# The offset convolution as four products per two columns, one on each strip of the array, in a bottleneck kernel with deformable sampling

## The chip, the cores and the metric

The kernel runs on one core of one Trainium2 chip. The metric is the device time in microseconds of one execution of the whole program. A profiled execution also has a span, from its first to its last instruction. TensorE (PE) multiplies matrices, VectorE (DVE) and ScalarE (ACT) do elementwise work and read PSUM, GpSimd (POOL) does elementwise work on SBUF, and SyncE (SP) issues the DMAs.

## The reference

The input is 64 images of 1024 channels by 14 x 14 points, in float32. Two residual blocks follow each other. The first is an ordinary bottleneck with batch normalisation. The second, where the change lies, is a bottleneck whose middle convolution samples its input at learned offsets:

```python
out = relu(group_norm(conv(x, w1)))                    # 1x1, 1024 -> 256 channels
om = conv(out, w_off, pad=1) + b_off                   # 3x3, 256 -> 27 channels: the offset convolution
off_x, off_y, mask = om[:, :9], om[:, 9:18], sigmoid(om[:, 18:])
py, px = grid_y + off_y, grid_x + off_x                # one point for each of 9 taps
sampled = bilinear_sample(out, py, px) * mask          # 9 samples for each output point
out = einsum('bckhw,ock->bohw', sampled, w2)           # 9 x 256 -> 256 channels
out = relu(group_norm(out))
out = relu(group_norm(conv(out, w3)) + x)              # 1x1, 256 -> 1024 channels
```

## The kernel before

Images go in 32 pairs: one tile has 128 channels on the partitions and two images of 196 points (392 columns) in a row. The first block takes about the first third of the span. After it `build_second_bottleneck` runs with `path = BANDED`: the 14 output rows fall into three groups (rows 0 to 6, 6 to 8, 8 to 14), and the nine taps into two sets, `tapsets` 0 with five taps and 1 with four. (`FULL`, for offsets of more than two points, is in the program and is not taken here.)

The second block is a pipeline over pairs. `fill` does the front work of pairs 0 and 1 and most of that of pair 2; then `slot(t)` runs for t = 0 to 31. In a slot in the middle, in this order on PE:

- `d1`: `first_conv` of pair t+1, 16 products of 392 columns (L1057).
- `sp[0]` woven with the first half of `d3`: `sampling` of pair t for tap set 0 (L1277) and `third_conv` of pair t-1 (L1412). Sampling multiplies the transposed activations `aT` with a matrix of weights `S`, which says how much of each source point each sample takes. `third_conv` makes 4 blocks j of 7 products m of 196 columns. ACT copies a bank to E (m = 1, L1416); DVE adds V from the next (m = 3, L1419); POOL adds twice from V (m = 4, L1424); DVE adds the results z at m = 5 (L1426) and m = 6 (L1431), and takes the group statistics of both results by `third_stats` (L953) right behind each.
- `om`: `offset_conv` of pair t+1 (L1102), then `selection`.
- `sp[1]` woven with the rest of `d3`: `sampling` for tap set 1, then the last two blocks of `third_conv`.
- `pd[0]` and `pd[1]`: `second_conv` of pair t over the samples, 36 products of 392 columns (L1306), with the normalisations, transposes, `factors` and `residual` put between them.

PE's order is this written order. Between `fill` and the last slot, the order on DVE, ACT, POOL and of the DMAs on SP comes from a planner with costs of its own; `keep_in_program_order` keeps marked instructions of an engine in the written order.

The offset convolution has 27 output channels, padded to 32, so it needs only a strip of 32 columns of the 128 x 128 array. There are 18 products (two halves of the channels, nine taps) of all 392 columns, and successive ones go to successive strips, so four partial sums lie in four quarters of a PSUM bank from the pool `ps`, which has three banks and also serves `first_conv`, `third_conv` and the transposes. The products read a zero-bordered copy `pad` of the activations, which POOL makes behind the ReLU on ACT (L1080, L1089). ACT and DVE add the four quarters (L1112, L1114, L1117).

The sampling weights come out of `om`: over several DMAs and elementwise steps, `factors` leaves distances `wd` in DRAM; `spread` broadcasts them into S (weights over rows, L1239) and X (weights over columns, L1235), three DMAs each for a tap set; `corners` multiplies S by X on DVE (L1257), and `sampling` takes the product. `lend` copies parts of `aT` (L1210), `store` writes z out (L1503), and `load` brings pair t+2 (L195, L201). The samples go to the tiles `sm0` and `sm1`, which ACT writes (L1285) and `second_conv` reads.

Of the kernel before, what the change touches and what calls it, by code (L numbers as in the profile page):

```python
# [10 lines left out]
FP = mybir.dt.float32  # L11
AF = mybir.ActivationFunctionType
ALU = mybir.AluOpType
# [31 lines left out]
def kernel(  # L45
# [818 lines left out]
    make_identity(nc, ident)  # L864


    woff_sb = const.tile([P, MB, T, 32], FP, tag="woff", name="woff_sb")
    nc.gpsimd.memset(woff_sb, 0.0)
    for c in range(MB):
        nc.sync.dma_start(woff_sb[:, c, :, :27], woff[ts(c, P)])  # L870
    boff_sb = const.tile([P, 1], FP, tag="boff", name="boff_sb")
    nc.gpsimd.memset(boff_sb, 0.0)
    nc.sync.dma_start(boff_sb[:27], boff)
# [18 lines left out]
    def build_second_bottleneck(l1, path, run, early):  # L892
# [36 lines left out]
        for s in range(2):  # L929
            for h0, h1, _ in groups:  # L930
                for i in range(2):
# [1 line left out]
                        base_sb[:, s, cols(h0, h1)].rearrange("p (i q) -> p i q", i=2)[:, i],  # L933
                        rows(base[:, s, :], h0, h1)[:, i].rearrange("(k r) q -> r k q", k=T),
                    )
        pad = one.tile([P, MB, 2, H + 2, W + 2], FP, tag="pad", name=f"pad{run}")
        nc.gpsimd.memset(pad, 0.0)

        class Norm:

# [132 lines left out]
        def first_norm(p):  # L1073
            q = pairs[p]

            def relu(c, i):
                n, a1 = q["gn1"], q["a1"]

                tc.keep_in_program_order(
                    nc.scalar.activation(  # L1080
                        a1[:, c, ts(i, HW)],
                        a1[:, c, ts(i, HW)],
                        AF.Relu,
                        bias=n.sh[:, c, i : i + 1],
                        scale=n.sc[:, c, i : i + 1],
                    )
                )
                if i == 1:
                    nc.gpsimd.tensor_copy(pad[:, c, :, 1 : H + 1, 1 : W + 1], images(a1[:, c, :]))  # L1089

            return [lambda: q["gn1"].mean(), lambda: q["gn1"].finish()] + [
                lambda c=c, i=i: relu(c, i) for c in range(MB) for i in range(2)
            ]

        def offset_conv(p):
            q = pairs[p]

            def step(n):
                if n == 0:
                    q["po"] = ps.tile([P, N2], FP, tag="ps", name=f"om_{p}")  # L1100
                c, k = divmod(n, T)
                nc.tensor.matmul(  # L1102
                    images(q["po"][ts(n % 4, 32), :]),
                    woff_sb[:, c, k, :],
                    window(pad, c, k),
                    start=(n < 4),
                    stop=(n >= MB * T - 4),
                )
                if n == MB * T - 1:

                    om = one.tile([P, N2], FP, tag="om", name=f"om_{p}")[:32]
                    nc.scalar.activation(om, q["po"][:32], AF.Identity, bias=boff_sb[:32])  # L1112
                    for j in (1, 2):
                        nc.vector.tensor_tensor(om, q["po"][ts(j, 32)], om, ALU.add)  # L1114
                    q["om"] = one.tile([32, N2], FP, tag="off", name=f"off_{p}")
                    for h0, h1, _ in groups:
                        nc.vector.tensor_tensor(  # L1117
                            q["om"][:, cols(h0, h1)].rearrange("p (i q) -> p i q", i=2),
                            rows(q["po"][96:], h0, h1),
                            rows(om, h0, h1),  # L1120
                            ALU.add,
                        )

            return [lambda n=n: step(n) for n in range(MB * T)]

        def selection(p):

# [25 lines left out]
        def factors(p):  # L1153
# [9 lines left out]
            def end():  # L1163
                wt = q["wt"]
                tc.keep_in_program_order(
                    nc.vector.tensor_tensor(wt[:, 0, :], wt[:, 0, :], q["mk"], ALU.mult)
                )

                q["wd"] = {}
                for s in (1, 0):  # L1170
                    for n, gs in alike.items():
                        if s:
                            t = dbounce.tile(
                                [2, len(gs), H, T, n], FP, tag=f"wd{n}", name=f"wd_{p}_{n}"
                            )
# [7 lines left out]
                q["S"], q["sm"] = {}, {}  # L1183

            return [distances, end]

# [34 lines left out]
                    yield g, r0, slice(off, off + n)  # L1221
                    off += n

        def spread(p, e):

            q = pairs[p]
            k0, k1 = tapsets[e]
            S, X = (
                one.tile([QR, wide * KT[e % 2]], FP, tag=f"{v}{e % 2}", name=f"{v}_{p}_{e}")
                for v in ("S", "X")  # L1230
            )
            for g, r0, piece in pieces(e):
                wd = q["wd"][g]
                shape = [R, W, piece.stop - piece.start]
                nc.sync.dma_start(  # L1235
                    X[:, piece],
                    wd[1, :, k0:k1, :].rearrange("r k n -> r (k n)").unsqueeze(0).to_broadcast(shape),
                )
                nc.sync.dma_start(  # L1239
                    S[:, piece],  # L1240
                    wd[0, r0 : r0 + R, k0:k1, :]
                    .rearrange("r k n -> r (k n)")
                    .unsqueeze(1)
                    .to_broadcast(shape),
                )
            q["S"][e] = S, X

        def corners(p, e):

            q = pairs[p]  # L1250
            S, X = q["S"][e]
            k0, k1 = tapsets[e]
            q["S"][e] = {}
            for g, r0, piece in pieces(e):
# [6 lines left out]
        def sampling(p, e):  # L1261
# [5 lines left out]

            def step(turn, g, h0, h1, chunks, c, i0, ni):
                if turn == 0:
                    q["sm"][e] = one.tile(  # L1270
                        [P, MB, KT[e % 2], 2, HW], FP, tag=f"sm{e % 2}", name=f"sm_{p}_{e}"
                    )
                n = (h1 - h0) * W
                pt = ps_s.tile([P, ni, kt, n], FP, tag="ps_s", name=f"sp_{p}_{e}_{g}_{c}_{i0}")
# [113 lines left out]
        def third_conv(p):  # L1388


            q = pairs[p]

            def step(j, m):
                if j == m == 0:
                    first_of_third(p)
# [24 lines left out]
                elif m == 4:  # L1420
                    V, E = q["V"], q["E"]

                    for o, b in ((E[:, 1], E[:, 1]), (z[1][:, HW:], V[:, 1])):
                        tc.keep_in_program_order(nc.gpsimd.tensor_tensor(o, V[:, 0], b, ALU.add))  # L1424
                elif m == 5:
                    nc.vector.tensor_tensor(  # L1426
                        z[0].rearrange("p (i n) -> p i n", i=2), bank, q["E"], ALU.add
                    )
                    third_stats(p, j)
                elif m == 6:  # L1430
                    nc.vector.tensor_tensor(z[1][:, :HW], bank[:, 1], q["V"][:, 0], ALU.add)  # L1431

                    tc.keep_in_program_order(third_stats(p, HB + j))

            return [lambda j=j, m=m: step(j, m) for j in range(HB) for m in range(7)]

# [97 lines left out]
        def slot(t):  # L1534
# [14 lines left out]
            d3 = part(back, third_conv, t - 1)  # L1549

            for e in range(2, E):
                sp[e - 2].append(lambda e=e: this and (spread(t, e), corners(t, e)))
# [13 lines left out]
            if d1:  # L1566
# [1 line left out]
                    d1, norm2 + weights[:1], (4, 7, 12, 12, 13, 13, 14, 10) if back else (10,)  # L1568
                )
                todo += put(weave(sp[0], d3[:half]), norm1, (4, 7, 14, 16, 18, 21))  # L1570
                todo += d3[half : half + 2]
                todo += put(om, weights[1:], (2,))
                todo += weave(sp[1], d3[half + 2 :])
            else:
                todo = put(sp[0], norm2 + weights[1:], (2, 5, 8, 9, 10, 10, 10, 7) if back else (7,))
                todo += put(weave(sp[1], d3[:half]), norm1, (1, 5, 10, 12, 14, 16))
                todo += put(d3[half:], om, (2,) * len(om))
            more = t + 2 < NP and not (early and t < 1)

            extra = [(3, s) for s in norm3[:1]]  # L1580
# [82 lines left out]
        def fill():  # L1663

            for p in range(3):
                start(p)
            load_h3(2, Z0)
            steps = first_conv(0, by_inputs=True)
            steps += put(
                first_conv(1),  # L1670
                first_norm(0) + [lambda: residual(2)] + offset_conv(0) + selection(0) + factors(0),
                (3, 6, 7, 7, 7, 7, 8) + (12,) * (MB * T) + (12, 16, 16),
            )
            steps += [lambda e=e: spread(0, e) for e in range(min(2, len(tapsets)))]
            steps += transposes(0, nc.scalar.copy) + [lambda: lend(0)]
            steps += put(
                first_conv(2),
                first_norm(1) + [lambda: corners(0, 0)] + offset_conv(1) + selection(1),
                (1, 4, 7, 7, 8, 8, 11) + (12,) * (MB * T) + (14,),
            )  # L1680
            for step in steps:
                step()
# [94 lines left out]
```

## Time and profile before

| what | value |
| --- | --- |
| time, median of 3 runs (lowest, highest) | 2985.78 us (2984.6, 2987.03) |
| the profiled execution: its time, its span | 2987.49 us, 2985.7 us |
| mean granted TensorE clock | 0.993 |
| busy: PE, DVE, ACT, POOL | 2926.6, 2069.0, 1191.8, 941.8 us |
| one slot in the middle, from the first product of L1057 to the next slot's | 61.39 us |
| of it busy: PE, DVE, ACT, POOL | 61.39, 38.79, 29.15, 13.95 us |

The busy time of a group is the time in which at least one of its instructions ran, so the mean duration of one instruction is longer than its share of the busy time where instructions overlap. One float32 product stands in the records as two matmuls. A line with an L is a line of the kernel before.

### The profile page before, as it was taken

What the parts mean: (1) busy time and instruction counts of PE and PEld (TensorE: products, weight loads), DVE (VectorE), ACT (ScalarE), POOL (GpSimd) and SP (SyncE); (2) the same over time, 40 slices, a digit from 0 to 9 for tenths busy, and PEclk for the clock granted to TensorE, in tenths of its full rate; (3) what the DMA queues carried; (4) which work ended last, traced back from release to release, by engine and by line L of the source; (5) the groups of instructions that cost most, each with busy time, mean ns of one, the idle gap of its engine ahead of it and who ended that gap; (6) DMA issues with size and microseconds to landing.
All of it is one profiled execution on the core that took longest, in us unless ns stands there. A gap on an engine that the chain in (4) does not pass through costs nothing.

```text
span 2985.7 us, 35773 instructions
## 1 busy us (share of the span) xinstructions
PE 2926.6 (98%) x11269; PEld 1821.8 (61%) x11269; DVE 2069.0 (69%) x5324; ACT 1191.8 (40%) x2504; POOL 941.8 (32%) x1004
## 2 busy tenths in 40 slices
PE   9999899989999999999999999999999999999997
PEld 5555555545555456666666666666666666666664
DVE  7877999997888456666566666666666665666655
ACT  0000222215555434445444454444444454444543
POOL 4621466655664012222222212222122222222121
PEclk9999999999999999999999999999999999999998
DMA  7654000015664436444554455444554445544531
GB/s 230 193 173 141 15 0 1 1 60 186 221 225 182 138 111 189 144 139 153 179 180 131 142 161 185 162 139 144 170 187 141 139 156 177 179 134 142 163 125 45
DMA packets 350411, 424.08 MB, mean 142 GB/s; under 512 B 27876, under 2 KB 292612, under 8 KB 349956
## 3 DMA queue, kind: packets, MB, share of 16 engines
q1 hardware_dynamic: 350212, 421.71, 43.6%
q8 instruction: 91, 1.49, 0.2%
q14 instruction: 108, 0.88, 0.1%
HBM read 296.63 MB, written 116.76 MB: 138 GB/s over the span
## 4 chain that ended last, share of the span: by engine, by line
PE 62%; DMA 1%; DVE 1%; SPq 0%; POOL 0%; ACT 0%; issue 0%; ACTq 0%; DVEq 0%; POOLq 0%
PE pd L1306 24%; PE sp L1277 13%; PE d L1057 10%; PE d L1412 10%; PE om L1102 3%; PE tr L1196 1%; DMA aT<-aT 1%; DMA S<-wd 0%; PE d L1460 0%; DMA wd<-wt 0%; POOL gn_0sc L1003 0%; SPq L1239 0%; DVE gn_0st L953 0%; PE gn_0p L978 0%; SPq L1235 0%
## 5 line engine op out<-in xcount | busy, mean ns | idle before, releaser
L1306 PE MATMUL pd<-sm,w2b_sb 128*128 128x392 f32 x2304 | 791.7, 494 | 0.0
L1306 PEld LDWEIGHTS pd<-sm,w2b_sb 128*128 128x128 f32 x2304 | 424.6, 190 | 267.9
L1277 PE MATMUL sp<-S,aT 126*128 126x420 f32 (+3 forms) x1536 | 490.7, 417 | 10.7 <-DVE S L1257 5.6
L1285 ACT COPY sm<-sp 128x336 f32<-128x336 f32 (+3 forms) x640 | 289.7, 453 | 257.5 <-PE sp L1277 249.2
L1057 PE MATMUL d<-h,w1b_sb 128*128 128x392 f32 x1024 | 357.2, 498 | 0.8 <-ACT h L224 0.8
L530 PE MATMUL c<-v,u_sb 128*128 128x392 f32 x1024 | 342.9, 497 | 11.0 <-DVE bn1sh L167 8.2
L530 PEld LDWEIGHTS c<-v,u_sb 128*128 128x128 f32 x1024 | 194.5, 191 | 159.3 <-issue 11.7
L1277 PEld LDWEIGHTS sp<-S,aT 126*128 126x128 f32 x1536 | 258.0, 191 | 25.7 <-ACT sm L1285 11.1
L1057 PEld LDWEIGHTS d<-h,w1b_sb 128*128 128x128 f32 x1024 | 189.2, 190 | 127.8 <-ACT h L224 2.9
L1493 ACT ACTIVATE z<-z,gn_0sh 128x196 f32<-128x196 f32 x504 | 182.7, 445 | 149.8 <-DVE gn_0sh L1019 134.0
L516 DVE TENSOR_TENSOR v<-t 128x392 f32<-128x392 f32 x256 | 193.1, 812 | 0.0
L1003 POOL TENSOR_TENSOR gn_0sc<-gn_0sc,mhalf 128x16 f32<-128x16 f32 (+3 forms) x35 | 94.6, 2702 | 285.6 <-DVE gn_0sc L1002 274.6
L1412 PE MATMUL d<-h,w3b_sb 128*128 128x196 f32 x744 | 180.4, 332 | 0.7 <-DVE z L1426 0.7
L1424 POOL TENSOR_TENSOR E<-V,E 128x196 f32<-128x196 f32 x124 | 74.1, 598 | 339.2 <-ACT sm L1285 186.7
L1485 DVE SCALAR_TENSOR_TENSOR z<-z,gn_0sc,h 128x196 f32<-128x196 f32 x504 | 178.5, 415 | 0.0
L1257 DVE TENSOR_TENSOR S<-S,X 126x840 f32<-126x840 f32 (+1 forms) x192 | 159.6, 883 | 25.1 <-DMA S<-wd 25.1
L1412 PEld LDWEIGHTS d<-h,w3b_sb 128*128 128x128 f32 x744 | 132.9, 189 | 51.5 <-issue 19.7
L953 DVE BATCH_NORM_STATS2 gn_0st<-z 128x6 f32<-128x196 f32 x504 | 157.4, 354 | 9.9 <-ACT z L1462 2.7
L385 PE MATMUL c<-xc,w1a_sb 128*128 128x392 f32 x384 | 149.1, 497 | 5.2 <-DMA xc<-in_x_dram 5.2
L224 ACT ACTIVATE h<-h,bn3sh 128x392 f32<-128x392 f32 x256 | 140.9, 622 | 11.6 <-DVE h L212 11.6
L212 DVE SCALAR_TENSOR_TENSOR h<-h,bn3sc,h 128x392 f32<-128x392 f32 x256 | 140.6, 620 | 0.0
L718 DVE BATCH_NORM_STATS2 st<-o 128x6 f32<-128x392 f32 x256 | 127.9, 555 | 14.9 <-ACT o L749 8.4
(810 smaller groups left out, 4345.0 us busy)
## 6 DMA issues: line engine op xcount, KB each, us to landing
xc<-in_x_dram SPq DMA_DIRECT2D x128, 392.0 KB
h<-o SPq DMA_DIRECT2D x64, 784.0 KB
h<-in_x_dram SPq DMA_DIRECT2D x64, 784.0 KB
h<-h SPq DMA_DIRECT2D x64, 784.0 KB
out_dram<-z SPq DMA_DIRECT2D x126, 392.0 KB
X<-wd SPq DMA_DIRECT2D x64, 413.4 KB
S<-wd SPq DMA_DIRECT2D x64, 413.4 KB
X<-wd SPq DMA_DIRECT2D x64, 330.8 KB
```

The costliest lines, as they stand in the source:

```text
L385: nc.tensor.matmul(acc[m], a, b, start=(j == 0), stop=(j == HB - 1))
L516: nc.vector.tensor_tensor(v[:, u].rearrange("p (i y x) -> p i y x", y=7, x=7), cols[c][:, :, i : i + 13 : 2, :], cols[c][:, :, j : j + 13 ...
L530: nc.tensor.matmul(m[u], u_sb[:, c, u, k % 4, ts(o, P)], vts[k][c][:, u], start=(c == 0), stop=(c == MB - 1),)
L953: last = nc.vector.bn_stats(self.st[:, b, i, :], src[:, ts(i, HW)])
L1057: nc.tensor.matmul(q["pt"][o], w1b_sb[:, c, ts(o, P)], q["y"][:, c, :], start=(c == 0), stop=(c == CB - 1),)
L1257: nc.vector.tensor_tensor(S[:, piece], S[:, piece], X[:, piece], ALU.mult)
L1277: nc.tensor.matmul(pt[:, i], q["aT"][:, i0 + i, c, starts.index(r0), :], q["S"][e][g, r0][:, :, i0 + i, :], start=(j == 0), stop=(j == len ...
L1285: nc.scalar.copy(dst, pt.rearrange("p i k n -> p k i n"))
L1306: nc.tensor.matmul(q["pd"][o], w2b_sb[:, c, k, ts(o, P)], q["sm"][e][:, c, k - k0].rearrange("p i q -> p (i q)"), start=(k == 0 and c == 0 ...
L1412: nc.tensor.matmul(bank[:, m % 2 if m < 6 else 1], a, b, start=(m < 6), stop=True, skip_group_check=True)
L1485: nc.vector.scalar_tensor_tensor(z[:, ts(i, HW)], z[:, ts(i, HW)], n.sc[:, b, i : i + 1], q["y"][:, o, ts(i, HW)], ALU.mult, ALU.add,)
L1493: nc.scalar.activation(z[:, ts(i, HW)], z[:, ts(i, HW)], AF.Relu, bias=n.sh[:, b, i : i + 1])
```

## The change

The offset convolution is written as F(2,3) along the width: for two neighbouring output columns and three taps of a row, four products of transformed inputs with transformed weights take the place of six. A product now has 98 column pairs of each of two images, 196 columns, for the middle row of taps and 182 for the other two; there are 24 instead of 18, and the four of one tap row go to the four strips. Their accumulators lie in a bank of `second_conv`'s (tag `pd0`) instead of one of `ps`.

`transform` makes the four transformed inputs of a channel half by four DVE instructions of 168 or 196 elements behind the ReLU, and a small POOL copy for the edge columns; the POOL copies to `pad` go. `offset_weights` transforms the weights once, by six DVE instructions, in `fill`. Behind the products ACT makes one copy of 196 columns with the bias, and DVE two additions of 196 columns and six smaller ones that write even and odd columns.

X and the transformed input u get no tiles of their own: X of a tap set goes to the start of that set's sample tile (`sm0`, `sm1`), and u to the second half of `sm1`. So `spread` is split. `spread_rows` brings S as before. `spread_columns` brings X, and its DMAs have to wait until `second_conv` has read the samples of the pair before: for tap set 1 it stands behind `pd[1]`, at the end of the slot. Lending and storing now come before that.

`third_conv` takes the statistics of block j at m = 4 of block j+1, and those of the last block at its end. In `slot` the second `corners` stands ahead of the third block of `third_conv` and of `om`, instead of behind the second product of `om`; in the slots without `d1` the order is put together anew.

The diff, cut; "..." marks what is left out.

```diff
-    woff_sb = const.tile([P, MB, T, 32], FP, tag="woff", name="woff_sb")
-    nc.gpsimd.memset(woff_sb, 0.0)
+    goff = const.tile([P, MB * T, 32], FP, tag="goff", name="goff")
+    woff_sb = const.tile([P, 4, MB * 3, 32], FP, tag="woff", name="woff_sb")
+    nc.gpsimd.memset(goff, 0.0)
     for c in range(MB):
-        nc.sync.dma_start(woff_sb[:, c, :, :27], woff[ts(c, P)])
+        nc.sync.dma_start(goff[:, ds(c * T, T), :27], woff[ts(c, P)])
+    def offset_weights():
+        g0, g1, g2 = (goff.rearrange("p (n k) o -> p n k o", k=3)[:, :, k] for k in range(3))
+        w1, w0, w2, w3 = (woff_sb[:, n] for n in range(4))
+        nc.vector.tensor_tensor(w0, g0, g2, ALU.add)
+        nc.vector.tensor_scalar(w0, w0, 0.5, None, ALU.mult)
+        nc.vector.scalar_tensor_tensor(w1, g1, 0.5, w0, ALU.mult, ALU.add)
+        nc.vector.scalar_tensor_tensor(w2, g1, -0.5, w0, ALU.mult, ALU.add)
+        nc.vector.tensor_scalar(w0, g0, -1.0, None, ALU.mult)
+        nc.vector.tensor_copy(w3, g2)
...
-        pad = one.tile([P, MB, 2, H + 2, W + 2], FP, tag="pad", name=f"pad{run}")
-        nc.gpsimd.memset(pad, 0.0)
...
+        shared = len(tapsets) == 2
+        transformed = {}
...
-                    nc.gpsimd.tensor_copy(pad[:, c, :, 1 : H + 1, 1 : W + 1], images(a1[:, c, :]))
+                    transform(p, c)
...
+        def room(p):
+            if p not in transformed:
+                if shared:
+                    t = sample_buffer(1, f"u_{p}")[:, wide * KT[1] :]
+                else:
+                    t = one.tile([P, MB * 4 * HW], FP, tag="U", name=f"u_{p}")
+                transformed[p] = t
+            return transformed[p].rearrange("p (c n i q) -> p c n i q", c=MB, n=4, i=2)
+        def transform(p, c):
+            u = room(p)[:, c]
+            rows = pairs[p]["a1"][:, c].rearrange("p (r w) -> p r w", w=W)
+            even, odd = rows[:, :, 0::2], rows[:, :, 1::2]
+            half = W // 2
+            for n, (j0, j1, a, b, op) in enumerate(
+                (
+                    (1, half, odd[:, :, 1:], odd[:, :, :-1], ALU.subtract),
+                    (0, half - 1, even[:, :, :-1], even[:, :, 1:], ALU.subtract),
+                    (0, half, even, odd, ALU.add),
+                    (0, half, odd, even, ALU.subtract),
+                )
+            ):
+                dst = u[:, n].rearrange("p i (h w) -> p (i h) w", w=half)
+                nc.vector.tensor_tensor(dst[:, :, j0:j1], a, b, op)
+            n = HW + half - 1
+            edge = u.rearrange("p n i q -> p (n i q)")[:, : 2 * n].rearrange("p (n q) -> p q n", n=2)
+            nc.gpsimd.tensor_copy(edge[:, : HW - 1 : half], rows[:, :, 1 : W - 1 : W - 3])
         def offset_conv(p):
             q = pairs[p]
+            half = W // 2
             def step(n):
+                c, k = divmod(n, 3)
+                k = (1, 0, 2)[k]
                 if n == 0:
-                    q["po"] = ps.tile([P, N2], FP, tag="ps", name=f"om_{p}")
-                c, k = divmod(n, T)
-                nc.tensor.matmul(
-                    images(q["po"][ts(n % 4, 32), :]),
-                    woff_sb[:, c, k, :],
-                    window(pad, c, k),
-                    start=(n < 4),
-                    stop=(n >= MB * T - 4),
-                )
-                if n == MB * T - 1:
+                    q["po"] = ps_d.tile([P, N2], FP, tag="pd0", name=f"om_{p}")[:, :HW].rearrange(
+                        "p (i q) -> p i q", i=2
+                    )
+                u = room(p)
+                o0, o1 = (half if k == 0 else 0), (H - 1 if k == 2 else H) * half
+                i0 = o0 + (k - 1) * half
+                for m in range(4):
+                    nc.tensor.matmul(
+                        q["po"][ts(m, 32), :, o0:o1],
+                        woff_sb[:, m, 3 * c + k, :],
+                        u[:, c, (2, 0, 3, 1)[m], :, i0 : i0 + o1 - o0],
+                        start=(n == 0),
+                        stop=(n == 3 * MB - 1),
+                    )
+                if n == 3 * MB - 1:
                     om = one.tile([P, N2], FP, tag="om", name=f"om_{p}")[:32]
-                    nc.scalar.activation(om, q["po"][:32], AF.Identity, bias=boff_sb[:32])
-                    for j in (1, 2):
-                        nc.vector.tensor_tensor(om, q["po"][ts(j, 32)], om, ALU.add)
+                    m1, m0, m2, m3 = (
+                        q["po"][ts(m, 32)].rearrange("p i q -> p (i q)") for m in range(4)
+                    )
+                    even, odd = om[:, :HW], om[:, HW:]
+                    nc.scalar.activation(even, m1, AF.Identity, bias=boff_sb[:32])
+                    nc.vector.tensor_tensor(odd, even, m2, ALU.subtract)
+                    nc.vector.tensor_tensor(even, even, m2, ALU.add)
                     q["om"] = one.tile([32, N2], FP, tag="off", name=f"off_{p}")
                     for h0, h1, _ in groups:
-                        nc.vector.tensor_tensor(
-                            q["om"][:, cols(h0, h1)].rearrange("p (i q) -> p i q", i=2),
-                            rows(q["po"][96:], h0, h1),
-                            rows(om, h0, h1),
-                            ALU.add,
-                        )
-            return [lambda n=n: step(n) for n in range(MB * T)]
+                        dst = q["om"][:, cols(h0, h1)].rearrange("p (i q n) -> p i q n", i=2, n=2)
+                        for n, (a, b, op) in enumerate(((even, m0, ALU.add), (odd, m3, ALU.subtract))):
+                            a, b = (
+                                v.rearrange("p (i q) -> p i q", i=2)[:, :, h0 * half : h1 * half]
+                                for v in (a, b)
+                            )
+                            nc.vector.tensor_tensor(dst[:, :, :, n], a, b, op)
+            return [lambda n=n: step(n) for n in range(3 * MB)]
...
-        def spread(p, e):
+        def sample_buffer(e, name):
+            t = one.tile([P, MB, KT[e % 2], 2, HW], FP, tag=f"sm{e % 2}", name=name)
+            return t.rearrange("p c k i q -> p (c k i q)")
+        def spread_rows(p, e):
             q = pairs[p]
             k0, k1 = tapsets[e]
-            S, X = (
-                one.tile([QR, wide * KT[e % 2]], FP, tag=f"{v}{e % 2}", name=f"{v}_{p}_{e}")
-                for v in ("S", "X")
-            )
+            S = one.tile([QR, wide * KT[e % 2]], FP, tag=f"S{e % 2}", name=f"S_{p}_{e}")
             for g, r0, piece in pieces(e):
-                wd = q["wd"][g]
-                shape = [R, W, piece.stop - piece.start]
+                nc.sync.dma_start(
+                    S[:, piece],
+                    q["wd"][g][0, r0 : r0 + R, k0:k1, :]
+                    .rearrange("r k n -> r (k n)")
+                    .unsqueeze(1)
+                    .to_broadcast([R, W, piece.stop - piece.start]),
+                )
+            q["S"][e] = S
+        def spread_columns(p, e):
+            q = pairs[p]
+            k0, k1 = tapsets[e]
+            n = wide * KT[e % 2]
+            if shared:
+                t = sample_buffer(e, f"X_{p}_{e}")
+                X = t[:QR, :n]
+                if e == 1:
+                    transformed[p + 1] = t[:, n:]
+            else:
+                X = one.tile([QR, n], FP, tag=f"X{e % 2}", name=f"X_{p}_{e}")
+            for g, r0, piece in pieces(e):
                 nc.sync.dma_start(
                     X[:, piece],
-                    wd[1, :, k0:k1, :].rearrange("r k n -> r (k n)").unsqueeze(0).to_broadcast(shape),
-                )
-                nc.sync.dma_start(
-                    S[:, piece],
-                    wd[0, r0 : r0 + R, k0:k1, :]
+                    q["wd"][g][1, :, k0:k1, :]
                     .rearrange("r k n -> r (k n)")
-                    .unsqueeze(1)
-                    .to_broadcast(shape),
-                )
-            q["S"][e] = S, X
+                    .unsqueeze(0)
+                    .to_broadcast([R, W, piece.stop - piece.start]),
+                )
+            q["X"][e] = X
...
+            def stats(j):
+                if j >= 0:
+                    third_stats(p, j)
+                    tc.keep_in_program_order(third_stats(p, HB + j))
...
+                    stats(j - 1)
...
-                    third_stats(p, j)
...
-                    tc.keep_in_program_order(third_stats(p, HB + j))
+                    if j == HB - 1:
+                        stats(j)
...
-                todo += d3[half : half + 2]
-                todo += put(om, weights[1:], (2,))
+                todo += weights[1:] + d3[half : half + 2] + om
                 todo += weave(sp[1], d3[half + 2 :])
...
-                todo = put(sp[0], norm2 + weights[1:], (2, 5, 8, 9, 10, 10, 10, 7) if back else (7,))
-                todo += put(weave(sp[1], d3[:half]), norm1, (1, 5, 10, 12, 14, 16))
-                todo += put(d3[half:], om, (2,) * len(om))
+                extra = list(zip((3, 6, 8, 9, 10, 10, 10), norm2)) + list(zip((0, 2, 4, 4, 5, 5), norm1))
+                extra = sorted(extra + [(9, w) for w in weights[1:]], key=lambda v: v[0])
+                todo = put(sp[0], [s for _, s in extra], [k for k, _ in extra])
+                todo += om + weave(sp[1], d3[:half]) + d3[half:]
...
-                todo += [lambda e=e: spread(t + 1, e) for e in range(min(2, E))]
-            if ahead:
-                todo.append(lambda: lend(t + 1))
+                todo += [lambda: spread_rows(t + 1, 0), lambda: spread_columns(t + 1, 0)]
+                todo += [lambda: spread_rows(t + 1, 1), lambda: lend(t + 1)]
             if back:
                 todo.append(lambda: store(t - 1))
...
             todo += put(pd[E - 1], extra, at)
+            if ahead:
+                todo.append(lambda: spread_columns(t + 1, 1))
...
```

More of the change, by code (lines that the diff above doesn't have):

```diff
@@ L1182, in end @@
                         )
-                q["S"], q["sm"] = {}, {}
+                q["S"], q["X"], q["sm"] = {}, {}, {}
             return [distances, end]
@@ L1235, in spread @@
                 nc.sync.dma_start(
                     X[:, piece],
-                    wd[1, :, k0:k1, :].rearrange("r k n -> r (k n)").unsqueeze(0).to_broadcast(shape),
-                )
-                nc.sync.dma_start(
-                    S[:, piece],
-                    wd[0, r0 : r0 + R, k0:k1, :]
-                    .rearrange("r k n -> r (k n)")
-                    .unsqueeze(1)
-                    .to_broadcast(shape),
-                )
-            q["S"][e] = S, X
+                    q["wd"][g][1, :, k0:k1, :]
@@ L1248, in corners @@
+                    .rearrange("r k n -> r (k n)")
+                    .unsqueeze(0)
+                    .to_broadcast([R, W, piece.stop - piece.start]),
+                )
+            q["X"][e] = X
         def corners(p, e):
             q = pairs[p]
-            S, X = q["S"][e]
+            S, X = q["S"][e], q["X"][e]
             k0, k1 = tapsets[e]
@@ L1269, in step @@
                 if turn == 0:
-                    q["sm"][e] = one.tile(
-                        [P, MB, KT[e % 2], 2, HW], FP, tag=f"sm{e % 2}", name=f"sm_{p}_{e}"
+                    q["sm"][e] = sample_buffer(e, f"sm_{p}_{e}").rearrange(
+                        "p (c k i q) -> p c k i q", c=MB, i=2, q=HW
                     )
@@ L1551, in slot @@
             for e in range(2, E):
-                sp[e - 2].append(lambda e=e: this and (spread(t, e), corners(t, e)))
+                sp[e - 2].append(lambda e=e: this and (spread_rows(t, e), spread_columns(t, e), corners(t, e)))
             d1 = part(front and not (early and t < 2), first_conv, t + 1)
@@ L1667, in fill @@
             load_h3(2, Z0)
-            steps = first_conv(0, by_inputs=True)
+            steps = first_conv(0, by_inputs=True) + [offset_weights]
             steps += put(
@@ L1671, in fill @@
                 first_norm(0) + [lambda: residual(2)] + offset_conv(0) + selection(0) + factors(0),
-                (3, 6, 7, 7, 7, 7, 8) + (12,) * (MB * T) + (12, 16, 16),
+                (3, 6, 7, 7, 7, 7, 8) + (12,) * (MB * 3) + (12, 16, 16),
             )
-            steps += [lambda e=e: spread(0, e) for e in range(min(2, len(tapsets)))]
-            steps += transposes(0, nc.scalar.copy) + [lambda: lend(0)]
+            steps += [lambda: spread_rows(0, 0), lambda: spread_columns(0, 0), lambda: spread_rows(0, 1)]
+            steps += transposes(0, nc.scalar.copy) + [lambda: lend(0), lambda: spread_columns(0, 1)]
             steps += put(
@@ L1678, in fill @@
                 first_norm(1) + [lambda: corners(0, 0)] + offset_conv(1) + selection(1),
-                (1, 4, 7, 7, 8, 8, 11) + (12,) * (MB * T) + (14,),
+                (1, 4, 7, 7, 8, 8, 11) + (12,) * (MB * 3) + (14,),
             )
```

## The prediction, on record before the run

> **What bounds the kernel now.** I read the page first, for the engines and the chain of waits.
>
> ```profile
> PE 2926.6 (98%) x11269; PEld 1821.8 (61%) x11269; DVE 2069.0 (69%) x5324; ACT 1191.8 (40%) x2504; POOL 941.8 (32%) x1004
> PE 62%; DMA 1%; DVE 1%; SPq 0%; POOL 0%; ACT 0%; issue 0%; ACTq 0%; DVEq 0%; POOLq 0%
> ```
>
> PE is busy for 98% of the span and carries the chain. The chain in order of time, around the offset convolution of one slot (columns: start, length, what):
>
> ```profile
> 1446.32 0.71 PE sp L1277 x2
> 1447.03 1.00 PE d L1412 x6
> 1448.03 3.42 PE om L1102 x36
> 1451.44 0.53 PE d L1412 x2
> 1451.97 0.57 PE sp L1277 x2
> ```
>
> There is no gap: a microsecond taken from `om` is a microsecond of the slot, unless a wait takes its place. 3.42 us for 36 matmuls is 0.095 each, though each lasts 0.492 (L1102). The timeline of the weight loads says why:
>
> ```profile
> 1447.95 0.16 PEld L1102 LDWEIGHTS om<-pad,woff_sb 128*32 128x32 f32 x8 [0.23 <-DVE z L1431]
> 1448.31 0.13 PEld L1102 LDWEIGHTS om<-pad,woff_sb 128*32 128x32 f32 x4 [0.20 <-issue]
> 1448.64 0.13 PEld L1102 LDWEIGHTS om<-pad,woff_sb 128*32 128x32 f32 x4 [0.20 <-issue]
> ```
>
> Four loads come within 0.13 us, then nothing for 0.20: the four strips run side by side, and a new four starts every 0.33 us, the time of 392 columns. The first line also has a wait for z: the next bank of `ps`.
>
> Next I read the vector engine, which gets the new work, in the same stretch:
>
> ```profile
> 1444.02 0.63 DVE L953 BATCH_NORM_STATS2 gn_0st<-z 128x6 f32<-128x196 f32 x2
> 1445.06 0.57 DVE L1419 TENSOR_TENSOR V<-d,E 128x392 f32<-128x392 f32 x1 [0.41 <-PE d L1412]
> 1446.43 0.57 DVE L1426 TENSOR_TENSOR z<-d,E 128x392 f32<-128x392 f32 x1 [0.81 <-POOL E L1424]
> 1447.03 0.63 DVE L953 BATCH_NORM_STATS2 gn_0st<-z 128x6 f32<-128x196 f32 x2
> 1447.58 0.34 DVE L1431 TENSOR_TENSOR z<-d,V 128x196 f32<-128x196 f32 x1
> 1447.96 0.63 DVE L953 BATCH_NORM_STATS2 gn_0st<-z 128x6 f32<-128x196 f32 x2
> 1448.50 1.91 DVE L1257 TENSOR_TENSOR S<-S,X 126x672 f32<-126x672 f32 x3
> ```
>
> It is nearly full from 1446.43 to 1450.41, and the `corners` that `sp[1]` needs (L1257) end under the cover of the 3.42 us of `om`. That cover shrinks. The windows view (us, then busy PE, PEld, DVE, ACT, POOL, clock, DMA share, GB/s) gives the whole stretch from the ReLU of the first channel half to the last statistics, and two stretches for the DMAs:
>
> ```profile
> 1444.65:1462.65 18.00, 18.00 (x106) 12.55 (x104) 12.17 (x32) 8.54 (x19) 4.49 (x8) 1.00 0.14 39
> 1442.66:1444.66 2.00, 2.00 (x10) 1.34 (x9) 1.92 (x6) 1.99 (x6) 0.00 (x0) 1.00 0.68 282
> 1444.66:1446.66 2.00, 2.00 (x10) 1.51 (x9) 0.80 (x2) 1.58 (x4) 1.41 (x3) 1.00 0.06 25
> ```
>
> The clock is full there, DVE has 5.8 us free of 18, and the DMA queues run dry at about 1444.7. Last, SP's own timeline:
>
> ```profile
> 1424.27 6.06 SPq L1503 DMA_DIRECT2D out_dram<-z  x4
> 1430.38 3.84 SPq L195 DMA_DIRECT2D h<-in_x_dram  x2
> 1434.32 4.32 SPq L201 DMA_DIRECT2D h<-h  x2
> ```
>
> **The products.** Before: eight fours and two twos, 10 starts of 0.329 = 3.29, and 0.13 to the next product, 3.42. After: 48 matmuls in 12 fours. Two matmuls of 196 columns take 0.33 (L1412 on the chain), so one start takes 0.165 at 196 columns and 0.153 at 182: 4 x 0.165 + 8 x 0.153 = 1.88, and the same 0.13: 2.01. Saved: 1.41 us a slot. The bound from the other side is a start every 0.19 (the LDWEIGHTS of L1412 last that long, those of L1102 0.109): 12 x 0.19 + 0.13 = 2.41, saved 1.0. I take 1.41: four loads need 0.13, less than 0.153. The bank wait (PE could go on at 1447.86, `om` starts at 1447.96) adds 0.10, as the bank `pd0` was read at 1423.4. In all 1.5 a slot. The new user of `pd0` has to be read before `pd[0]`: 9 us lie between.
>
> **The transforms and the order on DVE.** Eight DVE instructions of 168 or 196 elements with two SBUF inputs: the sixteen of L1485 (196, two SBUF inputs) follow each other every 0.34, so I take 0.34 and 0.30, 1.28 for a channel half, 2.56 a slot. (With stride 2, L504 takes 715 ns for 392, 0.36 for 196: little more.) Walk through 1444.65 to 1452 with these, in the written order: first half ready at 1444.65 (ACT L1080), its transform until 1445.93; V until 1446.50; the four statistics of block 0, now here, 4 x 0.31, until 1447.74; the second half (ReLU ends 1446.98) until 1449.02; two z until 1449.90; the first of three `corners` (0.76) until 1450.66. On PE: `om` starts at 1447.86, has done its first half at 1448.80, waits for the transform until 1449.1, ends at 1450.2 (0.94 + 0.13), one product until 1450.5, and `sp[1]` starts at 1450.8, behind `corners`. Before it started at 1451.81 (L1277 on PE). So 1.0 of the 1.5 is left; 0.5 goes to waits. Later in the stretch DVE has 12.17 + 2.56 + 1.24 (statistics moved in) = 16.0 us of work, in 18.0 - 1.0 = 17.0: it fits, but with 1.0 spare instead of 5.8, and part of that went in waits for POOL and PE. I take off 0.15: 0.85 a slot. Bounds: 1.5, if the planner puts the statistics into the idle 0.4 to 0.8 us; -0.7, if `corners` comes ahead of the second transform, for then `om` ends about 1.9 later.
>
> Beside POOL the transforms may be slower. L1358 and L1359 are the same POOL instruction, 1359 and 598 ns; the first runs beside the `corners` of tap set 0. POOL's additions (L1424) can lose as much, 0.76, but the z that needs them stands behind the second transform in the walk, so nothing is added. The Trainium skill, "SBUF — State Buffer", section "SBUF: two separate sides", calls the port pair that the two engines share an exclusive lock, taken whole by an instruction of DVE with two SBUF inputs or a POOL instruction that reads SBUF. By that rule a 0.6 us POOL instruction could also stop a transform: an estimate of 0.6 us once a slot would leave 0.25 instead of 0.85, and the sum would be 2975.
>
> The edge copies on POOL (L1089, 0.51 for 392 elements, is their upper bound) run beside the transforms: nothing. The additions behind `om` are about 1.8 us of DVE instead of 2.0: nothing. `offset_weights` is six instructions once, beside `first_conv`: nothing; uncovered, 2 us.
>
> **X moved.** Its three DMAs (0.74 each on SP, L1235) go behind `pd[1]`, which ends at 1424.66. SP has the stores before them; the whole queue is 2.2 us earlier, so stores go out until 1428.2 and X until 1430.4, ahead of 3.1 MB of loads (L195, L201), which then stand where they stood. X is 0.77 MB. At the 280 GB/s of these stretches it lands near 1436; behind the loads, with the queue's end, at 1444.7 or, at most, 2.8 later (0.77 MB more). `corners` wants it at 1449.9. Nothing lost. X of tap set 0 waits for `pd[0]`, near 1475, instead of 1468.95, and is wanted at 1493: nothing.
>
> **The ends.** 29 slots have this form: 29 x 0.85 = 24.7. In slot 1 `om` stands alone on PE (1.4). In slot 0 PE waits 1.70 us for `aT` (L1277, DMA), whose copies are issued 2.2 us earlier: 1.2. In `fill` the shorter `om` less the longer transform, on the way to the first weights: 0.5. Sum 27.8; bounds 0 to 5 for the three. Span 2985.7 - 27.8 = 2957.9. This execution was 1.8 longer than its span and 1.7 above the median of the runs, so the forecast for the median is 2958.
>
> **Rivals.** (1) DVE is no limit and PE keeps all 1.5: 29 x 1.5 + 5 = 48, 2937. For it: 5.8 us free on DVE; against it: the walk. (2) DVE gives all back, 2986: needs 0.85 more in waits, as from V and z late behind transforms. (3) Slower: X lands too late. `sp[1]` cannot start before X + 0.76 + 0.1; that equals the old 1451.81 when X lands at 1450.95, 26.3 us behind `pd[1]`. Each us beyond costs 29. At 28.0 it is 1.7 x 29 = 49: 3035. Against it: the dry queue at 1444.7; for it: these DMAs wait in the busiest stretch, and nothing in the trace shows them there. (4) The fours don't run side by side at half length: 48 x 0.109 = 5.2 instead of 3.42, 52 us more, 3038; against it, the loads above. (5) `corners` first: 0.7 x 29 = 20 more, 3006.
>
> **The numbers.** A measurement tells about 0.2% here, 6 us. Forecast, gains of 0.2 to 1.3 a slot: 0.55. Rival 1: 0.17; both are faster, 0.72 together. Rival 2, the same: 0.08. Slower: 0.20 (rival 3 0.12, 4 and 5 0.04 each). The range goes from rival 1, 2937, over rival 2 to 2990; it holds the forecast and rivals 1 and 2, 0.80.
>
> **What would show it.** `om` near 2.0 us on PE, with a wait for the transform's line of about 0.3; a wait of `sp[1]` for `corners` of about 0.3; no wait of L1257 for a DMA; a slot near 60.5. It is wrong if DVE waits for X, if `om` stays above 3 us, or if the slot is not shorter than 61.39.

## The result, and the profile after

The changed kernel took 2966.02 us (median of 4 runs, 2962.2 to 2966.53), the kernel before 2986.24 us (4 runs): a ratio of 0.993, 95% interval 0.9913 to 0.9947. It is 20 us faster; 28 were forecast, and the time lies in the range. Lines with an L are now those of the changed kernel: `first_conv` L1072, `transform` L1136, `om` L1160, the additions behind it L1175 to L1187, the mask of `selection` L1199, `corners` L1339, `sampling` L1359 with its copies L1367, `second_conv` L1388, `third_conv` L1500.

The page, engines and chain:

```profile
PE 2891.8 (98%) x11653; PEld 1829.8 (62%) x11653; DVE 2133.3 (72%) x5682; ACT 1180.9 (40%) x2504; POOL 934.5 (32%) x1003
PE 83%; DVE 10%; DMA 2%; ACT 2%; issue 1%; SPq 1%; POOL 0%; ACTq 0%; DVEq 0%; POOLq 0%
```

PE has 34.8 us less to do, but the span is only 21.0 shorter (2985.7 to 2964.7). A slot in the middle, from one first product of `first_conv` to the next, takes 60.51 us instead of 61.39. The chain in order of time shows what it gained and where it lost (start, length, what):

```profile
1445.35 1.00 PE d L1500 x6
1446.34 2.04 PE om L1160 x48
1448.38 0.53 PE d L1500 x2
1448.91 0.58 PE sp L1359 x2
1449.56 0.45 ACT sm L1367
1450.02 0.35 DVE om L1176
1450.94 0.58 DVE V L1507
1452.96 0.53 ACT mask L1199
1453.49 0.33 ACT sm L1367
1453.86 0.70 PE sp L1359 x4
```

`om` takes 2.04 us instead of 3.42, with no gap before it. But behind it the chain leaves PE, which it does nowhere in the slot of the kernel before that the prediction reads: over DVE's additions and the mask on ACT to a copy of samples, and back. ACT's timeline:

```profile
1451.31 0.44 ACT L1367 COPY sm<-sp 128x336 f32<-128x336 f32 x1 [0.46 <-PE sp L1359]
1452.96 0.53 ACT L1199 ACTIVATE mask<-off 32x392 f32<-32x392 f32 x1 [1.21 <-DVE off L1187]
1453.40 0.65 ACT L1367 COPY sm<-sp 128x336 f32<-128x336 f32 x2
```

The timeline of PE has the fourth product of `sp[1]`, and the one that had to wait:

```profile
1451.45 0.73 PE L1359 MATMUL sp<-S,aT 126*128 126x336 f32 x2
1453.86 0.70 PE L1359 MATMUL sp<-S,aT 126*128 126x112 f32 x4 [0.24 <-ACT sm L1367]
```

The fourth product ended at 1452.18, but its copy ran only behind the mask, which waited 1.21 us for DVE. Sampling has two PSUM banks in this kernel, so PE waits for the copy. DVE's timeline says why the mask's input is late:

```profile
1448.03 1.15 DVE L1339 TENSOR_TENSOR S<-S,X 126x224 f32<-126x224 f32 x2
1449.11 0.88 DVE L968 BATCH_NORM_STATS2 gn_0st<-z 128x6 f32<-128x196 f32 x3
1450.02 0.35 DVE L1176 TENSOR_TENSOR om<-om,om 32x196 f32<-32x196 f32 x1
1450.30 0.34 DVE L968 BATCH_NORM_STATS2 gn_0st<-z 128x6 f32<-128x196 f32 x1
1450.58 0.34 DVE L1177 TENSOR_TENSOR om<-om,om 32x196 f32<-32x196 f32 x1
1450.94 0.57 DVE L1507 TENSOR_TENSOR V<-d,E 128x392 f32<-128x392 f32 x1
1451.54 1.38 DVE L1187 TENSOR_TENSOR off<-om,om 32x84 f32<-32x84 f32 x6
```

ACT had its part of `om` done at 1448.86, but `corners`, the postponed statistics and a V of `third_conv` share DVE with the additions, and the last of them ends at 1452.92, 4.5 us behind `om` (1448.38); before it was 3.2 (1451.45 to 1454.60).

Cutting both traces at the first product of `first_conv` in the second block and in each slot gives an account of the span:

| stretch | before | after | difference |
| --- | --- | --- | --- |
| first block (unchanged) | 968.0 | 970.0 | +2.0 |
| `fill`, slots 0 and 1 | 149.6 | 150.2 | +0.7 |
| slots 2 to 29 | 1719.2 | 1694.3 | -24.9 |
| slots 30 and 31, tail | 149.0 | 150.1 | +1.1 |

The first block's length varies by itself: it was 967.2 to 970.0 in the eight changed kernels profiled here, though the change leaves it alone. Slot 30 has the short form too, so slot 31 and the tail became 2.0 longer.

### The profile page after: what moved, and what is told of

It is laid out like the page before. It is cut to its first block, busy times and chain, and to the rows that moved or that the text cites. A ratio compares the mean times of both kernels' runs of the same rounds, so it can differ in the third digit from the quotient of the medians.

```text
span 2964.7 us, 37198 instructions
## 1 busy us (share of the span) xinstructions
PE 2891.8 (98%) x11653; PEld 1829.8 (62%) x11653; DVE 2133.3 (72%) x5682; ACT 1180.9 (40%) x2504; POOL 934.5 (32%) x1003
## 4 chain that ended last, share of the span: by engine, by line
PE 83%; DVE 10%; DMA 2%; ACT 2%; issue 1%; SPq 1%; POOL 0%; ACTq 0%; DVEq 0%; POOLq 0%
PE pd L1388 25%; PE d L1072 11%; PE sp L1359 11%; PE c L385 10%; PE c L766 9%; PE d L1500 8%; PE c L530 6%; DVE v L516 3%; PE om L1160 2%; DVE off L1187 1%; PE tr L1261 1%; DMA X<-wd 1%; PE c L731 1%; ACT sm L1367 1%; DVE V L1507 1%
## 5 line engine op out<-in xcount | busy, mean ns | idle before, releaser
L1388 PE MATMUL pd<-sm,w2b_sb 128*128 128x392 f32 x2304 | 791.7, 494 | 0.0
L1388 PEld LDWEIGHTS pd<-sm,w2b_sb 128*128 128x128 f32 x2304 | 424.6, 190 | 267.9
L1359 PE MATMUL sp<-S,aT 126*128 126x420 f32 (+3 forms) x1536 | 493.4, 418 | 22.6 <-ACT sm L1367 12.1
L1367 ACT COPY sm<-sp 128x336 f32<-128x336 f32 (+3 forms) x640 | 285.2, 451 | 265.0 <-PE sp L1359 236.4
L1072 PE MATMUL d<-h,w1b_sb 128*128 128x392 f32 x1024 | 357.2, 498 | 0.8 <-ACT h L224 0.8
L1359 PEld LDWEIGHTS sp<-S,aT 126*128 126x128 f32 x1536 | 255.1, 190 | 46.8 <-ACT sm L1367 32.8
L1072 PEld LDWEIGHTS d<-h,w1b_sb 128*128 128x128 f32 x1024 | 189.3, 190 | 126.9 <-ACT h L224 3.0
L1339 DVE TENSOR_TENSOR S<-S,X 126x840 f32<-126x840 f32 (+1 forms) x192 | 160.8, 888 | 38.0 <-DMA X<-wd 34.3
L1500 PE MATMUL d<-h,w3b_sb 128*128 128x196 f32 x744 | 180.4, 332 | 0.0
L1500 PEld LDWEIGHTS d<-h,w3b_sb 128*128 128x128 f32 x744 | 133.0, 189 | 50.4 <-issue 19.4
```

Source lines behind the costliest of these rows:

```text
L1072: nc.tensor.matmul(q["pt"][o], w1b_sb[:, c, ts(o, P)], q["y"][:, c, :], start=(c == 0), stop=(c == CB - 1),)
L1339: nc.vector.tensor_tensor(S[:, piece], S[:, piece], X[:, piece], ALU.mult)
L1359: nc.tensor.matmul(pt[:, i], q["aT"][:, i0 + i, c, starts.index(r0), :], q["S"][e][g, r0][:, :, i0 + i, :], start=(j == 0), stop=(j == len ...
L1367: nc.scalar.copy(dst, pt.rearrange("p i k n -> p k i n"))
L1388: nc.tensor.matmul(q["pd"][o], w2b_sb[:, c, k, ts(o, P)], q["sm"][e][:, c, k - k0].rearrange("p i q -> p (i q)"), start=(k == 0 and c == 0 ...
L1500: nc.tensor.matmul(bank[:, m % 2 if m < 6 else 1], a, b, start=(m < 6), stop=True, skip_group_check=True)
```

## The experiments

The mark in each is the middle slot (median of the slots 2 to 29, which agree within 0.03 us but for at most five of a kernel, up to 0.23 longer), together with the two ends: `fill` to slot 1, and the rest from slot 30 on. After: 60.51, 150.2 and 150.1. All but the last of the kernels below were timed once.

**The mask behind more copies** (`mask_late`). `selection` is written behind the fifth product of `sp[1]`, and the planner is held to the order of the mask and these copies:

```diff
-                todo += weights[1:] + d3[half : half + 2] + om
-                todo += weave(sp[1], d3[half + 2 :])
+                todo += weights[1:] + d3[half : half + 2] + om[:-1]
+                todo += put(weave(sp[1], d3[half + 2 :]), om[-1:], (10,))
...
-                nc.scalar.activation(mask, om, AF.Sigmoid)
+                tc.keep_in_program_order(nc.scalar.activation(mask, om, AF.Sigmoid))
...
+                if e == 1:
+                    tc.keep_in_program_order(copied)
```

> Only the order on ACT is changed in the middle slots: the mask (Sigmoid) comes behind the fifth copy of samples instead of behind the third. Theory A (0.50 of the 1.38 us that the products save is lost because the mask waits on ACT for the last additions behind om, and the copies of samples wait behind the mask): the slot falls from 60.51 to 60.0 us, and the idle of ACT ahead of the mask goes. Theory B (DVE is simply too full behind om, so PE would wait whatever stands on ACT): the slot stays at 60.4 to 60.5 and PE's wait appears at third_conv or at the group statistics.

Measured: slot 60.01, the ends 150.6 and 148.8; 2950.16 us (one run; the kernel before took 2987.32 beside it). ACT in this kernel:

```profile
1448.62 0.44 ACT L1367 COPY sm<-sp 128x336 f32<-128x336 f32 x1 [0.46 <-PE sp L1359]
1449.38 0.34 ACT L1367 COPY sm<-sp 128x224 f32<-128x224 f32 x1 [0.33 <-PE sp L1359]
1449.63 0.52 ACT L1199 ACTIVATE mask<-off 32x392 f32<-32x392 f32 x1
```

The mask no longer waits, and in this stretch every copy that waits does so for PE. 0.50 us a slot came back, and 61.39 - 60.01 = 1.38 is all that `om` lost. Theory A holds; B is out, for DVE has the same work here.

**X in tiles of its own** (`own_x`).

```diff
-            if shared:
-                t = sample_buffer(e, f"X_{p}_{e}")
-                X = t[:QR, :n]
-                if e == 1:
-                    transformed[p + 1] = t[:, n:]
-            else:
+            if True:
                 X = one.tile([QR, n], FP, tag=f"X{e % 2}", name=f"X_{p}_{e}")
```

> X gets tiles of its own again; u stays in the second half of sm1, the order of issues is that of the change. Theory A (in the middle slots X arrives in time, but it is late in slots 0 and 1 and in the last one): the middle slots stay at 60.51 us within 0.05; fill to slot 1 is 3 to 5 us shorter, the last slot 1 to 2 us. Theory B (X in the busiest stretch of the DMA queues costs something in every slot): the slot falls by 0.2 us or more.

Measured: slot 60.50, `fill` to slot 1 145.9 (4.3 less), the rest 148.3 (1.8 less); 2959.32 us, one run. So waiting for the sample tiles costs nothing in the middle slots and 4.3 us at the start. What it costs at the end isn't settled: `corners_late`, with X in the sample tiles, has 148.8 there and not 150.1, and the same edit on top of `mask_late` takes the rest from 148.8 only to 148.6 (`mask_own`). In the changed kernel the chain runs through X at both ends; slot 1's start and the last slot's:

```profile
1057.34 8.93 DMA X<-wd
1066.36 1.03 DVE S L1339
```

```profile
2878.12 2.14 SPq L1592
2880.26 0.05 issue
2880.31 0.03 SPq L1321
2880.34 0.03 issue
2880.37 8.21 DMA X<-wd
```

In slot 1 the sampling weights are needed right away, with no `first_conv` in front. In the last slot the same, and X stands behind the stores (L1592) as well. 8 to 9 us from issue to landing are nothing beside 24 us of `first_conv` and the first sampling, but show where those are absent. Slot 0 pays too: at the start of its sampling PE waits 6.38 us for `corners` and 2.87 for a copy of samples; with X in its own tiles these are 7.12 and, again for `corners`, 0.16. In the last slot of `own_x`, X is still on the chain, and DVE waits 3.07 us for it.

**Statistics at once** (`stats_at_once`).

```diff
-                    stats(j - 1)
...
+                    third_stats(p, j)
...
-                    if j == HB - 1:
-                        stats(j)
+                    tc.keep_in_program_order(third_stats(p, HB + j))
```

> third_conv takes its statistics right behind each result again; all else as in the change. Theory A (the planner puts statistics into idle time wherever the program has them): the slot moves by less than 0.2 us from 60.51. Theory B (the later statistics are what makes room for the transforms, as the walk of the prediction has it): om or sp[1] waits for DVE and the slot is 60.9 us or more.

Measured: slot 60.77, the ends 150.8 and 151.3; 2972.91 us, one run. Between the two expectations: the postponement is worth 0.26 us a slot, and its place is the one in the prediction's walk, `sp[1]` behind `corners`, for which PE waits 0.53 us a slot here. ACT:

```profile
1449.48 0.44 ACT L1367 COPY sm<-sp 128x336 f32<-128x336 f32 x1 [1.65 <-DVE S L1339]
1450.15 0.44 ACT L1367 COPY sm<-sp 128x336 f32<-128x336 f32 x1 [0.23 <-PE sp L1359]
1451.05 0.44 ACT L1367 COPY sm<-sp 128x336 f32<-128x336 f32 x1 [0.46 <-PE sp L1359]
1452.14 0.53 ACT L1199 ACTIVATE mask<-off 32x392 f32<-32x392 f32 x1 [0.66 <-DVE off L1187]
```

Copies into `sm1` wait for all three `corners`, since X lies there; the mask then waits less (0.66 instead of 1.21), so part of one wait only takes the place of the other.

**The old convolution in the new kernel** (`old_conv`). `pad`, 18 products of 392 columns and the old additions come back; shared tiles, late statistics, new order and the bank `pd0` stay:

```diff
-                    transform(p, c)
+                    nc.gpsimd.tensor_copy(pad[:, c, :, 1 : H + 1, 1 : W + 1], images(a1[:, c, :]))
...
-            return [lambda n=n: step(n) for n in range(3 * MB)]
+            return [lambda n=n: step(n) for n in range(MB * T)]
```

> The convolution of before (18 products of 392 columns from the padded copy) in the changed kernel: X in the sample tiles, late statistics, the new order and the bank of second_conv stay. Theory A (the whole gain of the middle slots comes from the shorter products): the slot is 61.3 to 61.9 us, at or above the 61.39 of before. Theory B (the new order and the later statistics give part of it): the slot is 61.1 us or less.

Measured: slot 61.39, `fill` to slot 1 154.2, the rest 152.3; 2995.89 us, one run. All that the middle slots gain is the convolution's; the other parts give them nothing by themselves and cost 4.7 and 3.3 us at the ends against the kernel before. With `pd0` instead of `ps`, `om` starts 23.46 us into the slot, as in the kernel before and in the changed one: the bank gained nothing.

**Each transform twice** (`twice`).

```diff
-                nc.vector.tensor_tensor(dst[:, :, j0:j1], a, b, op)
+                for _ in range(2):
+                    nc.vector.tensor_tensor(dst[:, :, j0:j1], a, b, op)
```

> Every transform instruction on DVE is issued twice (the second writes the same values), 2.4 us more on DVE in each slot, nothing on PE. DVE is busy 14.18 of the 17.13 us from the first ReLU to the last statistics in the changed kernel. Theory A (the transforms nearly fill what DVE has free, so more work shows at once): om and sp[1] wait, the slot is 61.3 to 62.3 us. Theory B (DVE has room where it matters, the only loss is the mask's place on ACT): the slot is 60.8 us or less.

Measured: slot 62.47, just beyond theory A's end, the ends 157.3 and 153.0; 3029.59 us, one run. The transforms of the two halves take 2.19 and 2.18 us instead of 1.15 and 1.20, so DVE has 2.0 us more, not 2.4, and the slot is 1.96 longer. 1.82 of it is `om` (0.64 later, 1.18 longer). PE, DVE and POOL in this kernel:

```profile
1524.59 1.47 PE L1161 MATMUL om<-X,woff_sb 128*32 128x196 f32 x26
1526.72 1.15 PE L1161 MATMUL om<-X,woff_sb 128*32 128x196 f32 x22 [0.67 <-POOL X L1141]
1523.24 2.18 DVE L1137 TENSOR_TENSOR X<-a 128x168 f32<-128x168 f32 x8
1523.49 2.40 POOL L1513 TENSOR_TENSOR E<-V,E 128x196 f32<-128x196 f32 x1 [0.47 <-DVE V L1508]
1526.39 0.28 POOL L1141 COPY X<-a 128x56 f32<-128x56 f32 x1
```

`om` starts late because V of `third_conv` comes behind the longer transforms on DVE: PE waits 0.37 us for it. It is longer for another reason. The second transforms end at 1525.42, but the second half of `om` waits for the edge copy on POOL. That copy takes 0.28 us by itself; it stands behind an addition of `third_conv` that took 2.40 us beside the transforms instead of 0.60 (see the last section). So the larger part of the loss comes through POOL's queue, which neither theory has, and the run doesn't show how little room DVE itself had left.

**`corners` at its old place in the program** (`corners_late`).

```diff
-                todo += weights[1:] + d3[half : half + 2] + om
+                todo += d3[half : half + 2] + put(om, weights[1:], (2,))
```

> The second corners is written behind the second tap row of om again, as before the change; it issues nothing on PE. Theory A (the planner orders DVE by its own times, the place in the program matters little): the slot is 60.4 to 60.6 us. Theory B (the new place is needed): sp[1] waits for corners and the slot is 60.8 us or more.

Measured: slot 60.50; 2963.84 us, one run. The planner puts DVE in the same order either way as far as the slot can show. The ends are 149.4 and 148.8, 0.8 and 1.3 less than in the changed kernel; why stays open, and differences of this size at the ends of one execution prove little.

**Both mends together** (`mask_own`): the edits of `mask_late` and `own_x`.

> The mask behind the fifth copy of samples, and X in tiles of its own, in the changed kernel. Theory A (the two losses are separate): middle slots 60.0 us as with the mask alone, fill to slot 1 and the last slot as short as with X in its own tiles, in all about 2943 us, 43 us less than the kernel of before and 21 to 23 less than the change. Theory B (X in its own tiles gives the same waits back elsewhere): 2948 us or more.

Measured: 2944.99 us (median of five runs; four took 2943.27 to 2946.02, the fifth, left out of the ratio, 13739.83, and no trace says why), the kernel before 2988.66 (9 runs): ratio 0.985, interval 0.9835 to 0.9865. Slot 60.01, `fill` to slot 1 146.2, the rest 148.6: the loss of the middle slots and that of the start are separate. This version is faster than both kernels.

## Why the prediction was right, and where it was off

**The products** were right: 2.04 us measured against 2.01 forecast. Fours of 196 columns follow each other as fours of 392 do.

**The bank wait** (0.10) did not fall away. From the start of the last product of `third_conv` to that of the first of `om` it is 0.42 us (1445.85 to 1446.27), and 0.43 in the kernel before, where a product of `third_conv` takes 0.33: what the prediction put down to a bank is still there when the bank is another one.

**The net of a slot**, 0.85 forecast and 0.88 measured, is right because errors cancel, which is luck. The walk had 0.5 us lost ahead of `sp[1]` (the second transform, then `corners`); measured there is none. `om` starts as early in the slot as before and runs through. The walk put the four statistics of block 0 between the two transforms; the planner left all four ahead of the first (1441.42 to 1442.84 on DVE), 18.6 us into the slot, where they begin in the kernel before:

```profile
1441.42 0.37 DVE L968 BATCH_NORM_STATS2 gn_0st<-z 128x6 f32<-128x196 f32 x1
1441.96 0.88 DVE L968 BATCH_NORM_STATS2 gn_0st<-z 128x6 f32<-128x196 f32 x3
1442.99 1.15 DVE L1136 TENSOR_TENSOR X<-a 128x168 f32<-128x168 f32 x4 [0.15 <-ACT a L1095]
1445.88 1.20 DVE L1136 TENSOR_TENSOR X<-a 128x168 f32<-128x168 f32 x4
1447.27 1.92 DVE L1339 TENSOR_TENSOR S<-S,X 126x672 f32<-126x672 f32 x3
```

That comes to the walk's own better bound. And the 0.15 taken off for the stretch behind `om` was 0.50. The budget had 16.0 us of DVE work in 17.0; measured were 14.18 in 17.13, mostly because the 1.24 of statistics were not moved in. So it left 3 us, not 1, and still there was a wait, for a sum of work doesn't say who waits: the additions, late on DVE, held the mask, the mask held ACT's queue, and that held the copies. I wrote the additions off with "nothing", at 1.8 us instead of 2.0; the timelines have 2.07 instead of 1.87, but that is not the loss. I costed their work and not the queue behind the instruction that waits for them.

**X in the middle slots** was right. SP issued it at 1428.85 to 1431.3, behind the stores and ahead of the loads; `pd[1]` had ended at 1422.98; `corners` waits for a DMA of X nine times, 34.3 us in all, and only in slots 0, 1 and 31. Rival 3 named the right mechanism at the wrong place: it counts in those slots, which have no `first_conv` of a next pair ahead of the sampling.

**The ends** are the term that was mis-sized: 3.1 us of gain forecast, 2.7 of loss measured, leaving the first block aside. All of the forecast gain lay in `fill` and slots 0 and 1, where 0.7 was lost. I counted what is issued earlier (`aT`, whose wait of 1.70 us lies in slot 1, at 1064.62, and not in slot 0) and not what comes later there, X. With X in its own tiles this stretch is 3.6 us shorter than in the kernel before, near the forecast. Slot 31 and the tail, which I gave no term, lost the other 2.0; there the share of X is not settled.

So of the forecast 27.8, the slots gave 29 x 0.88 = 25.5, the ends took 2.7, and the unchanged first block happened to be 2.0 longer in this execution: 25.5 - 2.7 - 2.0 = 20.8 of the 21.0 in the span.

## What to carry to other kernels

When an engine's cover for others shrinks, follow the dependants of what it hid through each in-order queue: the loss here came through ACT, which got no added work, and one moved instruction brought all of it back. The lent buffer was free where the pipeline is full and was paid for at its first turns, so cost the first and last turns by themselves. A budget of busy time does not show where a wait will come.

## What the runs showed of the hardware that was not expected

Transforms (DVE, two SBUF inputs) and POOL's instructions meet here, and POOL loses. Its edge copies of 56 elements show it first. The copy's shortest is 281 ns; its median is 484 in the changed kernel and 1030, up to 1962, with each transform issued twice, while a transform's median is 355 and 356 ns. The one instruction's view, with each transform twice (durations are shortest, median, longest in ns):

```profile
L1141 POOL COPY X<-a x62: 281/1030/1962, 1008.8 to 2900.7; 128x56 f32<-128x56 f32 x62
```

In the slot of `twice` shown above, the addition L1513 takes 2.40 us beside eight transforms; its median is 0.597, and in the changed kernel, where in the slot shown it falls between the two runs of transforms, its longest is 0.602.

The Trainium skill's exclusive lock ("SBUF — State Buffer", section "SBUF: two separate sides") agrees with that in kind: POOL stands still. The 0.6 us by which a POOL instruction might have stopped a transform, in the prediction's sentence on the rule, was not seen: the longest transform of the second block's pipeline is 441 ns in the changed kernel, and through a run of transforms it was POOL that waited.
